# Giving the last addition of each softmax-denominator sum from GpSimd to an accumulating DMA

## The chip, the cores and the metric

The kernel runs on one core of a Trainium2 chip. The metric is the device time of one execution in microseconds (us), as the median of several runs. A profile is one further execution, recorded by the hardware profiler; its times are read from the records of each engine: TensorE (PE), VectorE (DVE), ScalarE (ACT), GpSimd (POOL) and SyncE (SP, which here only starts DMAs).

## The reference

The kernel computes one attention layer and one feed-forward layer with signed weights, each followed by a residual addition and a layer norm. All data are float32.

```python
# x: (4, 2048, 512), 16 heads of 32
q, k, v = (split_heads(x @ W.T) for W in (Wq, Wk, Wv))
energy  = einsum('nhqd,nhkd->nhqk', q, k)
attn    = softmax(energy / sqrt(32), axis=3)
out     = einsum('nhql,nhld->nhqd', attn, v)        # heads merged again
x = layernorm(x + out)
w = (weights >= 0) * 2 - 1
y = clip((x @ w.T) * scale + bias, -100, 100)
x = layernorm(x + y)
```

The change concerns one quantity only: the denominator of the softmax, the sum over the 2048 keys of exp(energy / sqrt(32) - maximum).

## The kernel before

**Tiles and loops.** The work is cut into 16 groups `n` (4 batches times 4 groups of 4 heads). A group has 4 query blocks `qb` of 512 queries, and each block has 16 steps `kc`, one for each chunk of 128 keys. So there are 64 blocks and 1024 steps, counted through by `s`. The main loop (L742) goes through them in order and issues for each step, engine by engine, what belongs to it:

- `scores` (L302): TensorE writes the maxima (L306) and adds the products of keys and queries (L312) into four PSUM banks, one for each head; ScalarE takes the exponential of the four banks (L319) into one tile `p` of 128 x 2048 float32, 1 MB. The tiles `p` come from `ppool`, which has 4 buffers, so step `s + 4` writes over the buffer of step `s`.
- `max_unit` (L236): for a block that is `LEAD` = 22 steps ahead, four products (L247) whose row maxima VectorE takes. The fourth bank is first copied by ScalarE to the tile `moved` (L266).
- fillers: projections (`piece`, L206), transposes, and the matmuls of the feed-forward layer (L510). A planner with estimated costs and due times (`plan`, L680) picks for each step which of them are issued.
- `weighted` (L323): on every second step, 8 matmuls (L330) that read two tiles `p`.
- `add_up` (L345): GpSimd sums the tiles `p` of a block into a tile `acc` of the same size, of which there are 2 buffers. For `kc` = 1 it writes `acc` as the sum of the first two tiles; for `kc` = 2 to 14 it adds one tile more (L350). This makes 14 additions of 128 x 2048 elements in a block. The tile of `kc` = 15 is not added; it is kept in `last_p`.
- `denominators` (L373): three steps after the block's last step, at `kc` = 2 of the next block, TensorE sums over the keys with a matrix of ones: four matmuls on `last_p`, four on `acc` (L356). ScalarE copies the result to `dT` (L382).

The last of the 64 blocks is different (`is_last`): GpSimd adds only the first half of its chunks, and TensorE does the rest.

**Order around the change.** [...]semaphores hold an instruction until what it reads is there and what it overwrites has been read. Three things wait for the last addition of a block (`kc` = 14). On ScalarE, the exponentials of `kc` = 2 of the next block write into the buffer of `p` that the addition reads. On TensorE, the four matmuls of L356 on `acc` read its result; they are issued at the same step, after that step's products of L312 and L247. On GpSimd, the next block's additions are queued behind it. SyncE starts the loads and stores to HBM; GpSimd starts no DMA in this kernel.

Of the kernel before, what the change touches and what calls it, by code (L numbers as in the profile page):

```python
# [14 lines left out]
ALU = mybir.AluOpType  # L15
# [5 lines left out]
def kernel(  # L21
# [11 lines left out]
    nc = tc.nc  # L33
# [10 lines left out]
    NT = S // P  # L44
# [130 lines left out]
    acc = {}  # L175
# [123 lines left out]
    def is_last(n, qb):  # L299
        return n == B * NG - 1 and qb == NQB - 1  # L300
# [42 lines left out]
        give(b, "DVE", 0.6)  # L343

    def add_up(n, qb, kc, p, before):  # L345
        if kc == 1:
            acc[n, qb] = apool.tile([P, HG, QB], F32, tag="acc", name="acc")
        if 0 < kc < (NT // 2 if is_last(n, qb) else NT - 1):
            a = acc[n, qb]
            nc.gpsimd.tensor_tensor(a, before if kc == 1 else a, p, ALU.add)  # L350
        if kc == NT - 1:
            last_p[n, qb] = p

# [275 lines left out]
    for n in range(N):  # L629
# [11 lines left out]
        for t in range(NT):  # L641
# [3 lines left out]
                 project_k, n, t, after=turned[b, i, j])  # L645
# [96 lines left out]
    while s <= max(*chosen, *behind):  # L742
        now = None
        if 0 <= s < total:
            n, at_n = divmod(s, STEPS)
            qb, kc = divmod(at_n, NT)
# [6 lines left out]
        if 0 <= s + LEAD < total:  # L753
            n, at_n = divmod(s + LEAD, STEPS)
# [16 lines left out]
        if now is not None:  # L771
            add_up(*now, before)
            before = now[3]
            held.append(now)
# [39 lines left out]
```

## Time and profile before

| | |
|---|---|
| median of 3 runs | 4421.93 us (4421.24 to 4422.01) |
| profiled execution | 4420.69 us, of which 4418.7 us are the span from the first to the last instruction |
| granted TensorE clock | 0.999 of full speed |
| busy time | TensorE 4380.8 us, GpSimd 4083.3 us, VectorE 3320.2 us, ScalarE 3048.4 us |
| additions on GpSimd (L350) | 825 of `acc<-acc,p` at 4537 ns and 64 of `acc<-p` at 4544 ns |
| DMA | 92.30 MB in all, 21 GB/s on average |

TensorE is busy for 99% of the span, but these ends are modelled, so a waiting TensorE can look busy. GpSimd is busy for 92%. The busy shares are averages over blocks that differ: the first batch has no feed-forward work beside it, the later ones have.

### The profile page before, as it was taken

The page shows a single profiled execution, that of the slowest core. Times are in us where ns is not written, and L with a number is a line of the kernel's source. Part 1 is how long each engine was busy: PE and PEld are TensorE (multiplying, and loading weights), DVE is VectorE, ACT ScalarE, POOL GpSimd, SP SyncE. Part 2 cuts the span into 40 slices and gives each one's busy share as a digit, 9 for nine tenths or more (in the row PEclk, how much of TensorE's full clock was granted, in tenths as well). Part 3 has the DMA queues.
Part 4 walks back from the last instruction along what each step waited for, and adds up shares of the span by engine and source line. Part 5 has one row for each costly group of instructions (what it writes and reads, how often), then busy time and mean ns, then how long its engine had stood idle before and what let it go on. Part 6 is the DMA issues. An engine that isn't in the chain of part 4 may idle for free.

```text
span 4418.7 us, 94451 instructions
## 1 busy us (share of the span) xinstructions
PE 4380.8 (99%) x38648; PEld 2261.4 (51%) x38648; DVE 3320.2 (75%) x5909; ACT 3048.4 (69%) x6493; POOL 4083.3 (92%) x940
## 2 busy tenths in 40 slices
PE   9999999999999999999999999999999999999998
PEld 5554444454555555555555555555555555555443
DVE  6777777777777777777777777777777777777774
ACT  5666666676667667677676766767667676767675
POOL 3999999999999999999999999999999999999994
PEclk9999999999999999999999999999999999999999
DMA  3000000010000000011000000001000000000001
GB/s 91 6 11 11 6 11 11 9 39 28 6 11 30 6 20 20 6 42 32 20 20 6 30 11 16 20 7 48 16 20 20 18 18 20 16 20 30 13 23 45
DMA packets 98019, 92.30 MB, mean 21 GB/s; under 512 B 4272, under 2 KB 73904, under 8 KB 97584
## 3 DMA queue, kind: packets, MB, share of 16 engines
q1 hardware_dynamic: 92304, 82.07, 6.2%
q8 instruction: 302, 4.95, 0.5%
q10 hardware_dynamic: 5280, 4.19, 0.3%
q14 instruction: 133, 1.09, 0.1%
HBM read 53.74 MB, written 32.51 MB: 20 GB/s over the span
## 4 chain that ended last, share of the span: by engine, by line
PE 89%; POOL 8%; ACT 1%; issue 1%; DVE 1%; DMA 0%; ACTq 0%; POOLq 0%; DVEq 0%
PE ps L330 19%; PE ps L247 18%; PE ps L312 18%; PE ps L206 15%; POOL acc L350 8%; PE ps L306 7%; PE ps L510 5%; PE ps L356 3%; PE ps L390 2%; PE ps L499 1%; PE ps L195 1%; ACT p L319 1%; DVE part L254 1%; PE ps L290 0%; ACT xg_last L489 0%
## 5 line engine op out<-in xcount | busy, mean ns | idle before, releaser
L350 POOL TENSOR_TENSOR acc<-acc,p 128x2048 f32<-128x2048 f32 x825 | 3743.2, 4537 | 106.1 <-ACT p L319 49.3
L319 ACT ACTIVATE p<-ps 128x512 f32<-128x512 f32 x4096 | 2115.0, 604 | 1148.4 <-PE ps L312 1113.8
L254 DVE TENSOR_REDUCE part<-ps 128x1 f32<-128x512 f32 x3072 | 1934.8, 684 | 821.1 <-PE ps L247 820.2
L247 PE MATMUL ps<-kT,qT 32*128 32x512 f32 x8192 | 1098.1, 590 | 0.0
L312 PE MATMUL ps<-qT,kT 32*128 32x512 f32 x8192 | 1070.7, 590 | 0.0
L330 PE MATMUL ps<-p,vv 128*32 128x512 f32 x8192 | 983.6, 598 | 0.5 <-ACT p L319 0.3
L247 PEld LDWEIGHTS ps<-kT,qT 32*128 32x128 f32 x8192 | 524.0, 185 | 379.8 <-issue 221.0
L254 DVE TENSOR_REDUCE part<-moved 128x1 f32<-128x512 f32 x1024 | 691.2, 675 | 1.7 <-ACT moved L266 1.6
L266 ACT COPY moved<-ps 128x512 f32<-128x512 f32 x1024 | 634.5, 620 | 21.8 <-PE ps L247 16.7
L330 PEld LDWEIGHTS ps<-p,vv 128*32 128x32 f32 x8192 | 220.3, 109 | 685.6 <-issue 346.5
L306 PE MATMUL ps<-negm,ones_bf 32*128 32x512 bf16 x4096 | 434.9, 384 | 3.9 <-ACT p L319 1.3
L312 PEld LDWEIGHTS ps<-qT,kT 32*128 32x128 f32 x8192 | 405.6, 184 | 38.3 <-issue 20.4
L350 POOL TENSOR_TENSOR acc<-p 128x2048 f32<-128x2048 f32 x64 | 290.8, 4544 | 132.4 <-ACT p L319 132.3
L342 DVE TENSOR_TENSOR oT<-ps,oT 128x512 f32<-128x512 f32 x448 | 309.8, 692 | 90.1 <-PE ps L330 57.6
L306 PEld LDWEIGHTS <-ones_bf 32*128 32x128 bf16 x4096 | 104.3, 91 | 496.9 <-issue 438.3
L206 PEld LDWEIGHTS ps<-wvT,xT 128*128 128x128 f32 x2048 | 244.6, 191 | 67.7 <-ACT p L319 62.1
L206 PE MATMUL ps<-wvT,xT 128*128 128x128 f32 x2048 | 270.3, 280 | 1.4 <-ACT p L319 0.5
L206 PEld LDWEIGHTS ps<-xT,wkT 128*128 128x128 f32 x2048 | 242.4, 191 | 48.2 <-ACT p L319 46.7
L206 PE MATMUL ps<-xT,wkT 128*128 128x128 f32 x2048 | 265.1, 279 | 0.5 <-ACT p L319 0.2
L206 PE MATMUL ps<-xT,wqT 128*128 128x128 f32 x2048 | 262.2, 277 | 1.1 <-ACT p L319 1.0
L510 PE MATMUL ps<-wsT,nT 128*128 128x172 f32 (+2 forms) x1408 | 259.3, 329 | 2.4 <-ACT nT L502 1.1
L206 PEld LDWEIGHTS ps<-xT,wqT 128*128 128x128 f32 x2048 | 245.2, 192 | 25.5 <-ACT p L319 23.0
(74 smaller groups left out, 1831.2 us busy)
## 6 DMA issues: line engine op xcount, KB each, us to landing
xs<-in_L_attn_x_dram SPq DMA_DIRECT2D x64, 256.0 KB, 2.8
xc<-in_L_attn_x_dram SPq DMA_DIRECT2D x60, 256.0 KB, 3.2
res<-xc SPq DMA_DIRECT2D x60, 256.0 KB, 2.4
xg<-res SPq DMA_DIRECT2D x12, 1024.0 KB, 6.1
out_dram<-xg SPq DMA_DIRECT2D x12, 1024.0 KB, 4.8
xg_last<-res SPq DMA_DIRECT2D x4, 768.0 KB, 6.1
out_dram<-xg_last SPq DMA_DIRECT2D x3, 1024.0 KB, 4.3
raw_wk<-in_L_attn_Wk_dram ACTq DMA_DIRECT2D x4, 256.0 KB, 6.3
```

Source lines behind the costliest of these rows:

```text
L206: nc.tensor.matmul(pp, lhsT=lhs(c), rhs=rhs(c), start=(c == 0), stop=(c == DC - 1))
L247: nc.tensor.matmul(ps[:, banks[h], :], lhsT=qT[n, qb][rows, ts(qc, P)], rhs=kT[n][rows, ts(kb, QB)], start=True, stop=True,)
L254: nc.vector.tensor_reduce(part[:, qc, h : h + 1, kb], src, AX.X, ALU.max, negate=True)
L266: nc.scalar.copy(moved, ps[:, banks[-1], :])
L306: nc.tensor.matmul(ps[:, banks[h], :], lhsT=ones_bf[rows, :], rhs=negm[n, qb][rows, :], start=True, stop=False,)
L312: nc.tensor.matmul(ps[:, banks[h], :], lhsT=kT[n][rows, ts(kc, P)], rhs=qT[n, qb][rows, :], start=False, stop=True,)
L319: nc.scalar.activation(p[:, h, :], ps[:, banks[h], :], AF.Exp, scale=SM_SCALE)
L330: nc.tensor.matmul(pb[cols, :], lhsT=vv[n][:, kc, cols], rhs=p[:, h, :], start=(i == 0), stop=(i == 1),)
L342: nc.vector.tensor_tensor(outs[n, qb], pb, outs[n, qb], ALU.add)
L350: nc.gpsimd.tensor_tensor(a, before if kc == 1 else a, p, ALU.add)
L356: nc.tensor.matmul(ps[h * HD : (h + 1) * HD, b, :], lhsT=ones, rhs=p[:, h, :], start=start, stop=stop,)
L510: nc.tensor.matmul(py, lhsT=self.nT[j][:, c, :], rhs=wT["ws"][:, c, cols], start=(c == 0), stop=(c == DC - 1),)
```

## The change

In each of the first 63 blocks the addition of `kc` = 14 (`NT - 2`) is no longer an instruction of GpSimd. GpSimd starts a DMA instead that reads the tile `p` and the tile `acc` in SBUF, adds them and writes the sum back to `acc`. The last block stays as it was. Nothing else is edited; the instructions of the other engines and their order are the same. The waits move with it: the matmuls on `acc`, and the exponentials that write over the buffer of `p`, wait for the completion semaphore of the DMA instead of GpSimd's. The first addition of the block after the next (the same buffer of `acc`) waits for it too. Lines after L345 are numbered one to three higher in the changed kernel: the additions are L351, the DMA L353, the matmuls with ones L359.

```diff
     def add_up(n, qb, kc, p, before):
+
         if kc == 1:
             acc[n, qb] = apool.tile([P, HG, QB], F32, tag="acc", name="acc")
-        if 0 < kc < (NT // 2 if is_last(n, qb) else NT - 1):
+        if 0 < kc < (NT // 2 if is_last(n, qb) else NT - 2):
             a = acc[n, qb]
             nc.gpsimd.tensor_tensor(a, before if kc == 1 else a, p, ALU.add)
+        elif kc == NT - 2 and not is_last(n, qb):
+            nc.gpsimd.dma_start(out=acc[n, qb], in_=p, accum_op=ALU.add)
         if kc == NT - 1:
             last_p[n, qb] = p
```

## The prediction

> **What bounds the kernel now.** I read the busy line first, then the chain, then stretches of the chain and the timeline at block ends, because the chain names two engines.
>
> ```profile
> PE 4380.8 (99%) x38648; PEld 2261.4 (51%) x38648; DVE 3320.2 (75%) x5909; ACT 3048.4 (69%) x6493; POOL 4083.3 (92%) x940
> ...
> PE 89%; POOL 8%; ACT 1%; issue 1%; DVE 1%; DMA 0%; ACTq 0%; POOLq 0%; DVEq 0%
> ...
> L350 POOL TENSOR_TENSOR acc<-acc,p 128x2048 f32<-128x2048 f32 x825 | 3743.2, 4537 | 106.1 <-ACT p L319 49.3
> ```
>
> TensorE carries 89% of the chain, the additions of L350 8%. GpSimd's 8% lie together. The chain restricted to 805 to 870 us is 98.3% POOL; restricted to 2279 to 2344 us it is all TensorE lines. GpSimd's own timeline in the early part shows why:
>
> ```profile
> 740.76 4.57 POOL L350 TENSOR_TENSOR acc<-p 128x2048 f32<-128x2048 f32 x1
> 745.40 59.90 POOL L350 TENSOR_TENSOR acc<-acc,p 128x2048 f32<-128x2048 f32 x13
> 805.26 4.57 POOL L350 TENSOR_TENSOR acc<-p 128x2048 f32<-128x2048 f32 x1
> ```
>
> One block takes 805.26 - 740.76 = 64.50 us, and GpSimd has no gap in it: 14 additions at 4.61 us (4.54 and a 0.07 us hand-over) are 64.5. So here GpSimd is the bound. It is so in some seven blocks (418 to 870 us). Later blocks take 66.5 to 70 us, and GpSimd idles 0.6 to 4 us at each boundary; there TensorE is the bound.
>
> How much could GpSimd's relief bring? From 547.2 to 805.2 us (four blocks at 64.5) TensorE is busy 255.14 of 258.00 us, 63.8 us a block. So 0.7 us a block, 5 us in seven blocks. The waits of TensorE on L350 are 3.3 us in the whole kernel, all at 4317 us. The ceiling of the gain is thus about 7 us, 0.16%. A measurement of this kernel tells about 0.2% (8.8 us) from no change.
>
> Now the other side: what waits for the last addition. The timeline at a boundary in the TensorE-bound part:
>
> ```profile
> 2334.85 9.14 POOL L350 TENSOR_TENSOR acc<-acc,p 128x2048 f32<-128x2048 f32 x2
> ...
> 2346.18 4.54 POOL L350 TENSOR_TENSOR acc<-p 128x2048 f32<-128x2048 f32 x1 [2.19 <-ACT p L319]
> ...
> 2348.33 2.06 ACT L319 ACTIVATE p<-ps 128x512 f32<-128x512 f32 x4 [0.97 <-PE ps L312]
> ...
> 2349.92 1.04 PE L356 MATMUL ps<-acc,ones 128*32 128x512 f32 x8
> ```
>
> The x2 are the additions of kc = 13 and 14. The 13th of the block ends at 2334.85 + 4.54 = 2339.39. The exponentials that write over the tile of kc = 14 start at 2348.33, the matmuls on `acc` at 2349.92. The DMA can start at 2339.39 (its tile was ready 4.5 us before), so it has a **window** of 8.94 us until ScalarE needs it and 10.53 until TensorE does. At the boundary of 805 us the window is much smaller: the 13th addition ends at 800.70, the exponentials start at 805.33, 4.63 us later.
>
> ```profile
> 805.33 2.07 ACT L319 ACTIVATE p<-ps 128x512 f32<-128x512 f32 x4 [1.60 <-POOL acc L350]
> ```
>
> [...]SyncE's 1 MB stores landed 4.8 us after issue[...]. [...]the trace has no adding DMA. [...]in the trace the additions last 4512 to 4560 ns whether DMAs run or not[...]. So I charge the DMA's traffic nothing on the other engines; were that wrong, a few us of transfer in 67 would be touched in each block.
>
> **The change part by part.**
>
> *Removed:* 63 additions on GpSimd, 63 x 4.61 = 290 us. In the TensorE-bound blocks they lie beside TensorE's work and are worth nothing; in the seven others at most 5 us, and about 2 us at 4317 us.
>
> *Added on GpSimd:* 63 DMA issues. Their cost on GpSimd itself is hidden: from the end of the 13th addition to the next block's first is 4.6 us (800.70 to 805.26) or more, most of which the 14th filled. SP's queue is not touched. The wait of the issue for kc = 14's tile costs nothing: that tile is ready 2.6 us or more before the 13th addition ends in every block. The wait of the next-but-one block's first addition is some 70 us old when it comes.
>
> *Moved:* the release of `p` and `acc`, from the end of the 14th addition (4.61 us after the 13th) to the landing of the DMA, D after the 13th. This is the term that decides.
>
> D is not in the trace, so bound it. [...]By the trace: stores landed in 4.8 us for 1 MB and 2.0 us for 256 KB, so 786 KB cost 2.8 us and 1 MB costs 3.7 us; a second source read puts 4.8 + 3.7 = 8.5. [...]I take **D = 9.0 us**. From above: reading, reading and writing one after another, 4.8 + 2 x 3.7 = 12.2.
>
> What does D cost? Behind the waiting exponentials ScalarE's queue holds the copy `moved` and the projections' copies, which free PSUM banks; TensorE stops at the matmuls on `acc` 1.6 us later. So the delay reaches TensorE, less a us or so. GpSimd then waits for the tile of kc = 2. That closes a ring: from the end of the exponentials of kc = 2, 0.2 us hand-over, 12 additions (kc = 2 to 13) at 4.61 = 55.3, D, and the next exponentials of kc = 2, 2.07. A block can't be shorter than **57.6 + D**, or than TensorE's own work. With D = 9.0 the floor is 66.6 us.
>
> I took the 63 distances between the products of kc = 2 of neighbouring blocks from the timeline. 16 of them are shorter than 66.6: five at 63.7 to 64.1, five at 64.5, one each at 65.0, 65.2, 65.4, 65.7, 65.8 and 66.0. Raised to 66.6 they cost 13.7 + 10.5 + 6.5 = 31 us. The other 47 (66.7 to 70.0) keep their time. All 16 lie in the first batch and at the start of the last group. The same sum for other D: 7 gives +4, 8 gives +15, 10 gives +57, 11 gives +106, 12.2 gives +175, 14 gives +289; below 6.1 it is -5. The curve is steep above 9.9, since from there all 63 blocks pay.
>
> Sum: the profiled execution of 4420.69 + 31 = 4452; it stands 1.2 us below the median of 4421.93, so **4453 us** as a median.
>
> **The rivals.**
>
> *The DMA fits the window.* It lands within 7.4 us or so[...]. Then no block pays much, and GpSimd's relief is kept: 4415 at best, 4430 at the point (D = 7.4) where the loss passes 0.2%. For it: the DMA engines are nearly idle (mean 21 GB/s), and no HBM is involved. Against it: the trace's plain 1 MB loads took 6.1 us already, with one source. To end faster by over 0.2% it would have to take the whole ceiling and more.
>
> *The adder is the slow part.* The DMA engines add float32 at half the stream's rate or worse[...]: D of 14, all blocks at 71.6 us, +289, 4710. From D = 12.3 on it decides. For it: nothing in the trace shows the adder.[...]
>
> *The waits cost nothing because TensorE has other work queued.* It has not: at the boundary it reaches the matmuls on `acc` within 1.6 us of the exponentials. This would only halve the 31 us, to about 4437.
>
> **How the numbers follow.** D between 7.4 and 12.3, slower: 0.68, with 4453 as its likeliest time and 4430 to 4600 as its range. D below 7.4: 0.18, of which 0.04 for a gain over 0.2% and 0.14 within it. D above 12.3: 0.14. The range runs from 4416, as the small gain costs it little, to 4610. Slower 0.68 + 0.14 = 0.82.
>
> **What the profile after would show.** 63 DMA issues on POOL with about 9 us to landing, and 63 additions fewer, at the same 4.54 us. Blocks from 418 to 870 us at about 66.6 us instead of 64.5, with ScalarE's exponentials of kc = 2 waiting for the DMA, and GpSimd idle at the block's third addition. Blocks after 1200 us as before. [...]Wrong would be: landings under 6 us (no block longer), landings over 12 us (every block longer), or other engines' instructions growing during the transfer.

## The result, and the profile after

The changed kernel takes 4467.27 us (median of 4 runs, 4461.98 to 4471.55) against 4421.59 us before: a ratio of 1.0103, 95% interval 1.0085 to 1.012. It is 46 us slower, about 1%. The profiled execution, the fastest of the four, took 4461.98 us, with a span of 4460.1 us, 41.4 us more than before.

The page of the changed kernel: busy line, chain by engine, the additions, and the new DMA (1024 KB each, 7.3 us from issue to landing in the median).

```profile
PE 4390.6 (98%) x38648; PEld 2262.9 (51%) x38648; DVE 3319.8 (74%) x5909; ACT 3049.3 (68%) x6493; POOL 3854.5 (86%) x940
...
PE 86%; POOL 6%; DMA 4%; ACT 2%; issue 1%; DVE 1%; ACTq 0%; POOLq 0%; DVEq 0%
...
L351 POOL TENSOR_TENSOR acc<-acc,p 128x2048 f32<-128x2048 f32 x762 | 3458.0, 4538 | 153.5 <-ACT p L319 104.2
...
acc<-p POOLq DMA_DIRECT2D x63, 1024.0 KB, 7.3
```

GpSimd lost 63 additions, some 286 us, and gained some 55 us for issuing the DMAs (63 at 0.88 us), so that it is busy for 229 us less; the remaining additions are as long as before. Yet the span grew: the chain now holds 4% of the DMA, against 0% before. Who waits for it is said by the line of the DMA (min, median and max of its time on GpSimd in ns; below, who waited, in us and times):

```profile
L353 POOL DMA_DIRECT2D acc<-p x63: 867/877/1073, 150.7 to 4349.4; - x63
...
  ACT p L319: 60.7, 23
  PEld ps L359: 5.7, 1
  PE ps L359: 4.8, 1
...
DMA to landing us min/median/max: 6.9/7.3/8.7
```

ScalarE sat idle before its exponentials until the DMA landed 23 times, 60.7 us in all. (The weight loads, PEld, and the matmuls, PE, show the same stop of TensorE twice; only the matmuls' is counted below.) One of these boundaries in the timeline, 676 to 700 us:

```profile
672.88 9.18 POOL L351 TENSOR_TENSOR acc<-acc,p 128x2048 f32<-128x2048 f32 x2
...
682.36 0.87 POOL L353 DMA_DIRECT2D acc<-p  x1 [0.30 <-POOL acc L351]
...
687.00 1.03 PE L247 MATMUL ps<-kT,qT 32*128 32x512 f32 x8
...
689.38 2.07 ACT L319 ACTIVATE p<-ps 128x512 f32<-128x512 f32 x4 [3.09 <-DMA acc<-p]
...
690.03 1.07 PE L359 MATMUL ps<-p,ones 128*32 128x512 f32 x8 [2.00 <-ACT p L319]
...
690.92 1.71 PE L359 MATMUL ps<-acc,ones 128*32 128x512 f32 x8
...
691.59 4.53 POOL L351 TENSOR_TENSOR acc<-acc,p 128x2048 f32<-128x2048 f32 x1 [1.71 <-ACT p L319]
692.38 2.99 PE L330 MATMUL ps<-p,vv 128*32 128x512 f32 x16
```

The 13th addition ends at 682.06; the DMA is issued 0.30 us later; the exponentials that need its buffer start at 689.38, 7.32 us after the 13th addition. ScalarE has sat idle for 3.09 us before them; where the landing is in time this is 0.91 us. TensorE's next matmuls wait for these exponentials, which empty PSUM banks, and stand still for 2.00 us. Then two matmul groups are longer than elsewhere: 1.71 us for 8 (1.07 just before), and 2.99 us for the 16 of L330 (1.92 at 680 us). That is the second loss, which the waits don't show: TensorE's clock. The columns below are length, busy time of PE, PEld, DVE, ACT, POOL, then the granted clock, for four blocks of the changed kernel:

```profile
484.40:550.20 65.80, 64.08 (x580) 31.64 (x580) 47.88 (x82) 44.27 (x95) 59.85 (x15) 1.00 0.12 25
550.20:615.90 65.70, 63.66 (x576) 31.39 (x576) 47.66 (x80) 44.20 (x94) 59.82 (x14) 1.00 0.11 25
615.90:682.10 66.20, 63.77 (x576) 31.50 (x576) 47.68 (x81) 44.20 (x94) 59.88 (x15) 1.00 0.11 25
682.10:749.50 67.40, 65.36 (x576) 31.74 (x573) 47.65 (x80) 44.20 (x94) 59.80 (x14) 0.97 0.11 25
```

The block with a clock of 0.97 is 1.2 to 1.7 us longer than its neighbours. The trace's clock record has a stretch of 3.41 us at half clock from 691.15 us, which costs half of it. The changed kernel has six such stretches ahead of its end, the kernel before none.

So the 41.4 us are accounted for: TensorE's shown waits at L359 are 31.6 us for ScalarE and 4.8 us for the DMA, against 3.2 and 1.2 at L356 before, 32.0 us more; six half-clock stretches make 6 x 1.7 = 10.2 us. The busy lines say the same: TensorE is busy for 9.8 us more (4390.6 against 4380.8) and stands still for 31.6 us more (69.5 of the span against 37.9), together 41.4. By place: the 13th addition of the 17th block ends at 1219.4 us instead of 1190.6, so 28.8 us are lost by the first 17 blocks; the 43 blocks up to 4140 us lose 5.4, the last ones 7.2.

### The profile page after: what moved, and what is told of

The parts are those of the page before. It is cut to its first block, busy times and chain, and to the rows that moved or that the text cites. A ratio compares the mean times of both kernels' runs of the same rounds, so it can differ in the third digit from the quotient of the medians.

```text
span 4460.1 us, 94517 instructions
## 1 busy us (share of the span) xinstructions
PE 4390.6 (98%) x38648; PEld 2262.9 (51%) x38648; DVE 3319.8 (74%) x5909; ACT 3049.3 (68%) x6493; POOL 3854.5 (86%) x940
## 4 chain that ended last, share of the span: by engine, by line
PE 86%; POOL 6%; DMA 4%; ACT 2%; issue 1%; DVE 1%; ACTq 0%; POOLq 0%; DVEq 0%
PE ps L330 19%; PE ps L312 17%; PE ps L247 17%; PE ps L206 14%; PE ps L306 7%; POOL acc L351 6%; PE ps L513 5%; DMA acc<-p 4%; PE ps L359 3%; PE ps L393 2%; ACT p L319 1%; PE ps L195 1%; PE ps L502 1%; DVE part L254 1%; PE ps L290 0%
## 5 line engine op out<-in xcount | busy, mean ns | idle before, releaser
L351 POOL TENSOR_TENSOR acc<-acc,p 128x2048 f32<-128x2048 f32 x762 | 3458.0, 4538 | 153.5 <-ACT p L319 104.2
L247 PE MATMUL ps<-kT,qT 32*128 32x512 f32 x8192 | 1098.0, 590 | 0.0
L330 PE MATMUL ps<-p,vv 128*32 128x512 f32 x8192 | 988.2, 600 | 0.5 <-ACT p L319 0.3
L247 PEld LDWEIGHTS ps<-kT,qT 32*128 32x128 f32 x8192 | 524.3, 185 | 379.4 <-issue 221.0
L330 PEld LDWEIGHTS ps<-p,vv 128*32 128x32 f32 x8192 | 221.9, 110 | 692.1 <-ACT p L319 344.1
L351 POOL TENSOR_TENSOR acc<-p 128x2048 f32<-128x2048 f32 x64 | 289.8, 4528 | 315.2 <-ACT p L319 315.2
L206 PEld LDWEIGHTS ps<-wvT,xT 128*128 128x128 f32 x2048 | 244.6, 191 | 67.7 <-ACT p L319 62.1
L206 PE MATMUL ps<-wvT,xT 128*128 128x128 f32 x2048 | 270.3, 280 | 1.4 <-ACT p L319 0.5
L206 PEld LDWEIGHTS ps<-xT,wkT 128*128 128x128 f32 x2048 | 242.4, 191 | 48.2 <-ACT p L319 46.7
L206 PE MATMUL ps<-xT,wkT 128*128 128x128 f32 x2048 | 265.1, 279 | 0.5 <-ACT p L319 0.2
L206 PE MATMUL ps<-xT,wqT 128*128 128x128 f32 x2048 | 262.2, 277 | 0.2 <-ACT p L319 0.2
L206 PEld LDWEIGHTS ps<-xT,wqT 128*128 128x128 f32 x2048 | 245.2, 192 | 24.2 <-ACT p L319 21.7
```

What stands on the lines that cost most here:

```text
L206: nc.tensor.matmul(pp, lhsT=lhs(c), rhs=rhs(c), start=(c == 0), stop=(c == DC - 1))
L247: nc.tensor.matmul(ps[:, banks[h], :], lhsT=qT[n, qb][rows, ts(qc, P)], rhs=kT[n][rows, ts(kb, QB)], start=True, stop=True,)
L330: nc.tensor.matmul(pb[cols, :], lhsT=vv[n][:, kc, cols], rhs=p[:, h, :], start=(i == 0), stop=(i == 1),)
```

## The experiments

Theory A holds the waits for the DMA's landing responsible, ScalarE's above all. Rival B names TensorE's matmuls on `acc` alone, rival C a cost of the DMA itself wherever it runs.

**e1: the matmuls on `acc` later.**

```diff
-            d = last + 2 if is_last(n, qb) else last + 3
+            d = last + 2 if is_last(n, qb) else last + 5
```

> The changed kernel with the denominators due two steps later (L668: last + 5 instead of last + 3), so that TensorE reads acc some 8 us later; the buffers of p are as they were. Theory A (the wait that costs is ScalarE's, the exponentials of kc = 2 that need the buffer of p back): nothing is taken away, 4455 to 4475 us, and about 60 us of ScalarE waiting for the DMA as in the changed kernel. Rival B (the wait that costs is TensorE's, the matmuls on acc): the cost goes, 4415 to 4430 us.

Measured: 4450.38 us (ratio to before 1.0064, 1.0049 to 1.0079), between the two theories. ScalarE's waits, and who now makes TensorE wait (us, times, longest):

```profile
ACT p L319 <- DMA acc<-p: 29.1, 12, 5.3
...
PE ps L330 <- ACT p L319: 16.7, 16, 2.3
```

Neither expectation held. More than half of the cost stays with the `p` buffer alone, but 17 us went with the matmuls. The later due time also has a price of its own: in e10 below, which has it without the DMA, the 43 blocks from 1200 us on take 4.6 us more than before. Its undisturbed fast blocks take 64.9 us (two of them, below) instead of 65.7, with the buffer wait still there: the matmuls on `acc` held up by the same landing had cost 0.9 us a block more. The granted clock was 0.997 to 0.998 in its four runs, against 0.994 to 0.997 in those of the changed kernel.

```profile
480.70:545.60 64.90, 64.12 (x576) 31.76 (x572) 47.74 (x81) 44.27 (x96) 59.90 (x15) 1.00 0.12 26
545.60:610.50 64.90, 64.07 (x576) 31.75 (x572) 47.68 (x81) 44.22 (x95) 59.86 (x14) 1.00 0.11 25
```

**e2: a fifth buffer for `p`.** The diff is shortened: four edits stand side by side.

```diff
-    stage = ... bufs=4      ppool = ... bufs=4      nT: bufs=4      for _ in range(4): load_x()
+    stage = ... bufs=3      ppool = ... bufs=5      nT: bufs=2      for _ in range(3): load_x()
```

> The changed kernel with a fifth buffer for p, so that ScalarE no longer needs the buffer of kc = 14 at kc = 2 of the next block but one step later; to make room, the x tiles have 3 buffers instead of 4 and nT 2 instead of 4. The denominators stay where they are. Theory A: ScalarE's wait for the DMA is gone; TensorE's matmuls on acc come 1.6 us later than the exponentials did, so that only some 1 us is left in the blocks of the first batch: 4418 to 4432 us, and no stretch at half clock. Rival B: still 4450 to 4470 us.

Measured: 4433.96 us (1.0027, 1.0018 to 1.0037), 2 us above the range of theory A and far from B. The waits for the DMA are now TensorE's own (the weight loads' and the matmuls' lines show the same stops):

```profile
PEld ps L359 <- DMA acc<-p: 23.6, 15, 6.0
...
PE ps L359 <- DMA acc<-p: 11.3, 11, 5.1
```

ScalarE's are gone, and TensorE's in the first batch are 1.3 us at most; the longest, 5.1 us, is at the last boundary. The granted clock of the profiled execution was 0.998, against 0.997 of the changed kernel and 0.999 before, so that some time at half clock, which was not expected, is left. Taking the buffer wait away removed 33 of the 46 us.

**e3 and e4: both waits taken away, with and without the DMA.** e3 has the edits of e1 and e2, e4 the same on the kernel before.

> The fifth buffer of p and the later denominators together, with the DMA. Theory A and rival B both: nothing waits for the DMA any more, and what is left is GpSimd's relief: 7 us under the same layout without the DMA (e4). Rival C (the DMA itself slows the engines or GpSimd's additions): slower than e4 by more than 5 us.

> The kernel before (14 additions on GpSimd, no DMA) with the same fifth buffer of p, 3 and 2 buffers for x and nT, and the denominators two steps later: the control of e3. GpSimd still makes 14 additions at 4.61 us in a block, so the blocks of the first batch stay at 64.5 us: 4418 to 4428 us.

Measured: e3 4423.10 us (1.0002, 0.9994 to 1.0011), e4 4423.90 us (1.0006, 0.9997 to 1.0014). With both waits gone nearly the whole loss is gone, and e3 with the DMA is not slower than e4 without it; rival C falls. But e3 is not 7 us ahead of e4, and e4's fast blocks are not at 64.5 us: TensorE's products of `kc` = 2 follow each other there at 64.02 us, while GpSimd goes on at 64.5 us (its 13th additions end at 418.68 and, seven blocks on, at 870.14). With a fifth buffer GpSimd may fall behind for these few blocks and catch up in the longer ones. The buffer gives what the DMA gives.

**e5: the addition left out.**

```diff
-            nc.gpsimd.dma_start(out=acc[n, qb], in_=p, accum_op=ALU.add)
+            pass
```

> The changed kernel without the DMA: the tile of kc = 14 is left out of the sum altogether in the first 63 blocks (this part of the computation is missing). It shows what GpSimd's relief is worth when nothing takes the addition's place. All theories: GpSimd makes 13 additions in a block, the blocks of 418 to 870 us fall from 64.5 to about 63.9 us and the wait at 4317 us goes: 4414 to 4418 us.

Measured: 4414.70 us (0.9984, 0.9977 to 0.9991). GpSimd's relief alone is worth 7.1 us.

**e6: a plain copy instead of the adding transfer.**

```diff
-            nc.gpsimd.dma_start(out=acc[n, qb], in_=p, accum_op=ALU.add)
+            nc.gpsimd.dma_start(out=acc[n, qb], in_=p)
```

> The changed kernel with a plain copy of p to acc by the same queue instead of the accumulating one (the sum is lost, only the tile of kc = 14 is left in acc). It measures what the second read and the adder cost. Theory A (an adding transfer costs a second read[...]): landing 4.4 to 5 us after issue instead of 7.3, which fits the windows, so 4416 to 4425 us. Rival D[...]: landing over 6 us, and 4430 us or more.

Measured: 4421.51 us (1.0, 0.999 to 1.0009), and a landing 4.7 us after issue, as theory A had it. Rival D, by which the copy would land late as well, falls.

```profile
acc<-p POOLq DMA_DIRECT2D x63, 1024.0 KB, 4.7
...
ACT p L319 <- DMA acc<-p: 7.3, 3, 3.7
```

The second read and the addition together cost 7.3 - 4.7 = 2.6 us of the landing; their shares were not measured. The copy's landing fits nearly all windows: all 46 us of the loss are gone, and the time is 7 us above that of e5.

**e7: the adding transfer twice, one after the other.**

```diff
-            nc.gpsimd.dma_start(out=acc[n, qb], in_=p, accum_op=ALU.add)
+            for _ in range(2):
+                nc.gpsimd.dma_start(out=acc[n, qb], in_=p, accum_op=ALU.add)
```

> The changed kernel with the accumulating DMA issued twice in each block (the tile of kc = 14 is then added twice); the second waits for the first, so the release comes some 15 us after the 13th addition instead of 7.6. Ring theory (block = 58.5 us + landing): every block becomes about 74 us, 350 to 420 us more than before. Clock theory (a TensorE that stands still for some us is set to half clock for 3.4 us): a stretch at half clock at most of the 63 boundaries, about 1.7 us each, so another 50 to 110 us. Together 4770 to 4950 us; without the clock's share 4770 to 4840.

Measured: 4991.51 us (1.129, 1.1267 to 1.1313; two runs), 42 us above the range. Every boundary waits, and the granted clock is lower, 0.949 in the mean and 0.93 in the stretch below:

```profile
PE 4515.2 (90%) x38648; PEld 2282.3 (46%) x38648; DVE 3319.2 (66%) x5909; ACT 3049.2 (61%) x6493; POOL 3907.5 (78%) x1003
...
ACT p L319 <- DMA acc<-p: 514.4, 63, 13.0
...
530.00:605.00 75.00, 66.04 (x582) 31.74 (x572) 48.01 (x82) 44.55 (x96) 60.74 (x16) 0.93 0.17 36
```

The span grew by 575 us, to 4993.8. Of these TensorE is busy for 134 us more (4515.2 against 4380.8), which is the clock's share, and stands still for 441 us more. Both are above what was expected, 50 to 110 and 350 to 420 us. The waits are longer because the 12 additions between two releases take 58.5 us here instead of the 56.2 of the changed kernel, so that a block takes 75.9 us on average and not 74. The clock's share is larger because more time was spent at half clock than the 3.41 us a boundary that I had counted. An estimate from the granted clocks: 0.949 of 4993.8 us against 0.999 of 4418.7 us is some 500 us at half clock more than before, 8 us a boundary. The 134 us that TensorE is busy for longer are 268 us of it; the rest, nearly half, falls where TensorE stands still anyway and costs nothing.

**e8: the DMA only where the windows are wide.**

```diff
+        by_dma = NG <= n < (B - 1) * NG + NG - 1
-        if 0 < kc < (NT // 2 if is_last(n, qb) else NT - 2):
+        if 0 < kc < (NT // 2 if is_last(n, qb) else NT - 2 if by_dma else NT - 1):
...
-        elif kc == NT - 2 and not is_last(n, qb):
+        elif kc == NT - 2 and by_dma:
```

> The accumulating DMA only in the blocks of groups 4 to 14 (44 blocks); the first batch and the last group keep 14 additions on GpSimd. Theory A (the cost lies where the window is small, in the first batch and at the end): 4421 to 4430 us. Rival C (each DMA costs some us wherever it is): two thirds of the 46 us, about 4452 us.

Measured: 4425.94 us (1.0009, 1.0 to 1.0017). 44 of the 63 DMAs cost 4 us (0 to 8 by the interval), and the first batch takes as long as before. ScalarE waits for the DMA 4 times, 7.0 us. The place decides, not the number.

**e9 and e10: another attempt at a faster version, and its control.** One `xc` buffer instead of two pays for the fifth buffer of `p`, and the x tiles keep four; otherwise as e3 and e4.

> The accumulating DMA with a fifth buffer of p and the denominators two steps later, as in e3, but the room comes from one xc buffer instead of two and two nT buffers, and the x tiles keep their 4 buffers, so that the start isn't delayed. Theory A: no wait for the DMA except at the last boundary, no half-clock stretch, the blocks of the first batch at 64.0 us: 4415 to 4420 us, the level of e5 within some us. Rival C (the DMA itself slows the engines): 4422 us or more.

> The control of e9: the kernel before, without the DMA, with the same buffers and due times. As e4 showed the blocks of the first batch at 64.0 us too, because GpSimd may fall further behind, it should be within 4 us of e9: 4415 to 4422 us. If it is 5 us or more above e9, the DMA has a gain of its own.

Measured: e9 4423.38 us (1.0003, 0.9994 to 1.0011), e10 4423.79 us (1.0005, 0.9997 to 1.0013). The expectation of e9 failed by 3 us, and e10's range by 2 us. By its time alone e9 lies where rival C put it, but e10 without the DMA is no faster, so the DMA is not the reason. Its fast blocks are at 63.96 us and only one boundary waits for the DMA (2.8 us). The gain goes elsewhere. The profiled execution of e9 is slower ahead of the first block: from 76.4 us on two matmul groups of 8 (L247, L206) take 2.50 and 2.08 us, and 1.55 and 1.16 us in the kernel before. The first block begins 4.3 us later (its first products at 88.16 instead of 83.87 us). e9's profiled execution was granted a clock of 0.998, e10's, its fastest run, 0.999. And the 43 blocks from 1200 us on take 4.1 us more than before in e9 and 4.6 us more in e10, without the DMA; e1, whose only edit is the due time, shows the same longer blocks (every fourth one 67.8 us instead of 67.3). The DMA brings no gain of its own in either pair, and no version here that computes the whole sum beats the kernel before.

## Why the prediction was right, point by point

The direction, the mechanism and the place were right, and 4467 lies within 4416 to 4610. That range was wide, from a small gain to a loss of 4%, so that lying in it says less than the mechanism does. The likeliest time, 4453, was 14 us short, and that it came so near is partly luck: three terms of the sum were off and partly cancelled.

**The ceiling of the gain, 7 us.** Confirmed by e5, 7.1 us, although one of its terms was read too large: the 3.3 us of waits at 4317 us are one stop of TensorE counted on its weight loads (2.1 us) and on its matmuls (1.2 us). That is why the change could not pay: it relieves an engine that was the bound in seven blocks of 64.

**GpSimd's own cost of the issue is hidden.** Confirmed: it took 877 ns, in the median, and began 0.30 us after the 13th addition at nearly every boundary, and the next block's first addition came 2 us or more after the 13th ended at every boundary, waiting for its tile and not for the issue.

**D = 9.0 us.** Too large. From the end of the 13th addition to the landing it was 7.2 to 9.0 us, 7.6 in the median. My 8.5 took 3.7 us for the second read, the slope of the stores to HBM; the adding transfer took 2.6 us more than the copy of e6. The copy landed in 4.7 us, near the 4.8 of the stores, so that 4.8 + 2.6 = 7.4 us would have met the 7.3 from issue. The 0.5 us on top of the 8.5 were an estimate of mine for GpSimd's part, with nothing of the trace behind it; the issue takes 0.88 us on GpSimd. The rival with a slow adder, which needs 12.3 us or more, is refuted.

**The ring, 57.6 + D.** Right in form, short by a term. With D = 7.25 it gives 64.85 us; e1, where the matmuls on `acc` are out of the way, has 64.83 to 64.88 in three blocks. In the changed kernel such blocks took 65.75. The 12 additions in the ring took 56.2 us instead of 55.3, because GpSimd waited for the tile of `kc` = 3 as well (0.96 us at 565 us); with the matmuls on `acc` later, in e1, they take 55.3. These matmuls, which I had placed as a wait 1.6 us later, stand in TensorE's queue ahead of the next scores. The prediction counted that wait as a limit to be reached later, not as work that the landing delays.

**What was not in the sum: the clock.** Six stretches at half clock, 10.2 us in the profiled execution. The run times spread from 4462 to 4472 us while the granted clock goes from 0.997 to 0.994; 0.3% of 4465 us is 13 us, so most of the spread goes with the clock. The trace is that of the fastest run; the median's further 5 us are seen in its clock alone.

**The 16 blocks.** The list and the sums are right, but not the remark that all 63 blocks pay from D = 9.9: about half of them are shorter than that floor of 67.5 us, and all only from D = 12.4. With D = 7.6 the curve gives some 10 us, with each boundary's own landing 12, where 41 came. The 0.9 us of the ring and the clock filled most of the gap, and the blocks from 416 to 883 us came out at 66.6 us on the mean, the very number predicted, for other reasons. Blocks after 1200 us were unchanged but for those where a landing was late (8.5 us in a window of 7.4 us at 2844 us), as far as the trace shows.

**Why landings scatter between 6.9 and 8.7 us** was not foreseen, and the trace goes far towards it. During 19 of the 63 transfers no packet of another DMA queue was in flight, and these landed 6.94 to 7.00 us after issue; the 44 others took 6.94 to 8.71. So every landing later than 7.01 us had company, often a single packet of 16 KB on a queue that the page lists as "instruction" (q8). That the company causes the delay was not tested.

**That the waits cost nothing because TensorE has other work.** Refuted, as argued: TensorE stood still for 32 us more.

## What to carry to other kernels

Here work moved from a busy engine to a DMA was paid in latency. Ask first what the relief is worth where that engine is the bound (here 7 us), and then who waits for the last result and for the buffers it reads, counting from the moment the transfer can start. The transfer that adds needed its copy's time, 4.7 us, and 2.6 us for the second read and the addition; where that does not fit the window, the iteration pays, unless the source has a spare buffer and the result is read later (e3). When a wait makes TensorE stand still, add the clock to the bill (here 10.2 of 41.4 us).

## What the runs showed of the hardware that was not expected

In the changed kernel's profiled execution some waits of TensorE of only two to three microseconds are followed by half clock for 3.41 us. In its first batch nine waits at L359 lasted 2.00 to 3.06 us; five of them were followed by such a stretch, which began between 0.2 us before the restart and 1.3 us after it, the four others (2.00 to 2.39 us) not; of the shorter ones there (0.56 to 1.70 us) none was. In e7, where the waits at this line are 7.0 us in the mean (433.5 us, 62 times), half clock comes to the 8 us a boundary estimated above.

Which waits are followed by it can be told apart in this trace. Its stretches, with the one at the kernel's end (4452.64 us), begin 78, 39, 20, 59, 956 (3263.142 us) and 28 times 3413.33 ns after one another, to within 5 ns. Cut into pieces along this grid, equal waits fall apart by the idle time inside one piece: the wait of 2.00 us at 688.03 lies in one piece, which ends at 691.15, where half clock begins; that of 2.39 us at 621.89 is divided into 1.00 and 1.39 and has no stretch. Without the first 85 and the last 100 us, I count the pieces at full clock that hold a part of a gap of over 0.25 us: the six in which TensorE idled for 2.00 us or more were followed by half clock, none of the 29 with 1.98 us or less (ends of matmuls as the profile models them). This is the count of one execution; what sets the clock was not shown. Idle time is not all of it: ahead of the first block a gap of 1.50 us was followed by full clock in the kernel before and in the changed one, and by the slower matmuls from 76.4 us on in e9. Why stays open.
